# Sixteen batches split into parts of 12 and 4 instead of 10 and 6 for the last layer, with new groups and a new group order

## Chip, core and metric

One core of one Trainium2 chip runs the whole program in one launch. The metric is the device time of that core in microseconds (us), the median of the runs shown; smaller is better. Engines: PE multiplies matrices, PEld loads its weights, DVE, ACT and POOL work on vectors, SP issues most DMAs. DMAs between memory and memory, or memory and the on-chip buffers, run on 16 DMA engines that all queues share.

## What is computed

Input `x` has 16 batches of 256 tokens with 256 features, in f32. Four layers follow one another, each adding to `x`: a cross-attention with 8 heads, a feed-forward layer with per-batch weights, a second cross-attention, and a mixture of 8 experts. Only the last one matters here:

```
x = x + _L1_ffn_ref(_layernorm(x, axis=-1), Wg, Wu, Wd, Wr, temperature)

inh = sigmoid(x @ Wr / temperature)                       # one number per token and expert
in_zone = (inh >= 0.5 - log(4/3)) & (inh <= 0.5)
w = exp(-abs(inh - 1/e) / 0.1) * in_zone                  # no expert in zone: the two nearest serve
h = silu(gate) * up ; e_out = h @ Wd ; out = sum over e of weights_e * e_out_e
```

The reference lets each expert work on each token, and weights the result. The weight is zero where the expert does not serve the token, so how many tokens an expert serves depends on the data.

## The kernel before, in words

**Attention and chains.** The loop at L1297 has 128 steps, one per batch and head, with the matmuls of the first attention. What follows for a batch (output projection, feed-forward layer, second attention, last layer norm: `chain`) and its routing (`route`) are generators. Function `gap` runs them between the matmuls of the loop, by a model of the time that PE needs, so the order of instructions on each engine is fixed when the program is built.

**Routing.** `route` counts with two small matmuls (`pn`, L699) how many tokens each expert serves. It keeps a running count `next_slot` for each part and expert. A part is a set of consecutive batches: `PARTS = (10, 6)` (L161), so part 0 has 2560 tokens and part 1 has 1536 (`NTOKS`). Each token has one slot in the list of each expert, in a DRAM tensor `slots_d` per part: a served token takes the next slot from the front, any other a slot from the end. POOL scatters the rows there (L718), 16 scatters of 128 rows per batch.

**Capacity.** `CAPS` (L163) is half the tokens of a part: 1280 slots for part 0 and 768 for part 1. Only these first slots of each list are worked on in the normal course. A tile is 128 slots, so there are 8 x 10 + 8 x 6 = 128 tiles.

**Expert groups.** `groups` cuts lists into groups of up to four tiles: (4, 3, 3) for part 0, (3, 3) for part 1, and (3, 2, 1) for the last expert of part 1. `experts` (L1229) works on them in the order of `lists`. For a group, three groups ahead, SP loads its rows (L1137). Two groups ahead DVE transposes 32x32 blocks (L291), and SP sends them to DRAM and fetches them back in turned order (L296, L302), which completes the transposition. Then come `gate` (`pg`) and `up` (`pu`) with tanh on ACT and two DVE operations (L1205, L1206). One group later, `down` (`pd`) is scaled by the token's weight on DVE (`o`, L1219), and POOL adds each tile into the output with one scatter (L1220). There are nine `o` buffers. Scatters of one part and expert, and scatters of different parts, may overlap; a scatter of the same part but another expert waits until those before it have landed.

The first two groups of the job are prepared by PE transposes (`rowsT`, L84) instead of that round trip. The job starts four steps before the end of the loop, beside the last chains; a load from part 1 is not issued until batch 15 has been routed.

**The guarded block.** At the end DVE compares the counts with the capacities (`more_d`, `most`, `beyond`, L1356 to L1358). All engines load the result into a register (L1359) and branch on it (L1360). If any expert of any part has more tokens than its capacity, the block at L1361 works on all remaining slots of all lists, from the capacity to the end:

```
        nc.vector.tensor_tensor(more_d, next_slot, limit, ALU.subtract)
        nc.vector.tensor_reduce(most, more_d.rearrange("p k e -> p (k e)"), AX.X, ALU.max)
        nc.vector.tensor_scalar(beyond, most, 0.0, None, ALU.is_gt)
        some = nc.values_load(beyond[0:1, 0:1], min_val=0, max_val=1)
        with tc.If(some > 0):
            drain(experts(groups(0, "+", (4, 3, 3)) + groups(1, "+", (3, 3))))
```

Of the kernel before, what the change touches and what calls it, by code (L numbers as in the profile page):

```python
# [29 lines left out]
def xattn_ffn_kernel(  # L30
# [16 lines left out]
    E = Wg.shape[0]  # L47
# [110 lines left out]
    )  # L158


    PARTS = (10, 6)  # L161
    NTOKS = [n * S for n in PARTS]
    CAPS = [n // 2 for n in NTOKS]  # L163

# [151 lines left out]
    def advance(gen):  # L316
        return gen is not None and next(gen, DONE) is not DONE

    def drain(gen):
        while advance(gen):  # L320
            pass
# [306 lines left out]
    def route(b, A, mine):  # L628
        while not mine.done or (b >= 1 and not A.tails[b - 1].done):
            yield 0.4  # L630
        part = 0 if b < PARTS[0] else 1
        row = A.row[b]
# [105 lines left out]
    with ExitStack() as sh, ExitStack() as sa, ExitStack() as sf:  # L738
# [377 lines left out]
        def load_expert(e):  # L1116
            k = len(D_.w)
            pool = D_.front if k == 0 else D_.wk if k == 1 else D_.more
            w = D_.w[e] = pool.tile([P, 3, DC, D], F32, bufs=1, name=f"wx_{e}")
            nc.sync.dma_start(w[:, 0], Wg[e].rearrange("(c p) i -> p c i", p=P))  # L1120
            nc.sync.dma_start(w[:, 1], Wu[e].rearrange("(c p) i -> p c i", p=P))
            nc.sync.dma_start(w[:, 2], Wd[e].rearrange("(c p) d -> p c d", p=P))
# [106 lines left out]
        def experts(groups, ready=None):  # L1229

            if groups[0].e not in D_.w:
                load_expert(groups[0].e)
            for g in groups[:2]:
                g.load()
            yield 7.0
            while D_.wk is None:
                yield 0.4
            for d in range(DC):
                groups[0].turn_rows(d)
                yield 2.0  # L1240
            late = None
            for n, g in enumerate(groups):
                if n == 0:
                    groups[2].load()
                if n + 3 < len(groups):
                    while ready is not None and not ready(groups[n + 3]):
                        yield 0.4
                for i in range(IC):
                    g.gate(i)
                    yield  # L1250
                    g.up(i)
                    yield
                    if n == 0:
                        groups[1].turn_rows(i)
                    if n + 2 < len(groups):
                        if i == 0:
                            groups[n + 2].send_rows()
                        else:
                            groups[n + 2].fetch_rows()
                    if i == 0 and n + 3 < len(groups):  # L1260
                        groups[n + 3].load()
                    if late is not None:
                        late.down(2 * i)
                        late.down(2 * i + 1)
                        yield
                ahead = groups[min(n + 3, len(groups) - 1)].e
                if ahead not in D_.w and (len(D_.w) < 2 or D_.more is not None):
                    load_expert(ahead)
                if n + 2 < len(groups) and groups[n + 2].e not in D_.w:
                    while D_.more is None:  # L1270
                        yield 0.4
                    load_expert(groups[n + 2].e)
                late = g
            for t in range(late.tiles):
                late.down(t)

        def groups(part, more, sizes, experts_=range(E)):

            gs = []
            for e in experts_:  # L1280
                t = CAPS[part] // P if more else 0
                for k in sizes:
                    gs.append(G(part, e, t, k, more))
                    t += k
                assert t == NTOKS[part] // P if more else t == CAPS[part] // P
            return gs

        first = groups(0, "", (4, 3, 3))  # L1290
        lists = (
            first[:-1] + groups(1, "", (3, 3), range(E - 1))
            + first[-1:] + groups(1, "", (3, 2, 1), [E - 1])
        )

        last = None
        for n in range(NS + 2):  # L1297
# [60 lines left out]
        nc.vector.tensor_scalar(beyond, most, 0.0, None, ALU.is_gt)  # L1358
        some = nc.values_load(beyond[0:1, 0:1], min_val=0, max_val=1)  # L1359
        with tc.If(some > 0):  # L1360
            drain(experts(groups(0, "+", (4, 3, 3)) + groups(1, "+", (3, 3))))  # L1361


# [36 lines left out]
```

## Time and profile before

| | us |
|---|---|
| median of 3 runs | 1845.71 (1845.11 to 1851.59) |
| profiled execution, its time | 1845.63 |
| its span, first to last instruction | 1843.6 |
| PE busy | 1808.7 (98%) |
| DVE busy | 1212.0 (66%) |
| POOL busy | 846.4 (46%) |
| ACT busy | 583.2 (32%) |

The profiled execution took 1845.63 us, 2.0 us more than its span. Busy PE time includes waits inside its pipeline. In lines that tell of waiting, the engine after the arrow is the one whose result came last; `issue` means that nothing which the profile shows was waited for. Names that end in q are the sequencers of an engine.

### The profile page before, as it was taken

How to read it: one execution, taken by the hardware profiler on the slowest of the kernel's cores; microseconds unless marked ns; L12 is line 12 of the kernel's file. 1: busy time of each engine (PE TensorE's matmuls, PEld its weight loads, DVE VectorE, ACT ScalarE, POOL GpSimd, SP SyncE). 2: the span in 40 equal slices, each digit the busy share in tenths (PEclk: the TensorE clock that was granted, in tenths of full speed). 3: DMA queues.
4: the chain of work that ended last, by engine and by line, in shares of the span. 5: the costliest groups of instructions: out<-in, count | busy, mean ns of one | idle time of the engine just before them, and what ended most of it. 6: DMA issues, size and time to landing. Idle time of an engine off the chain costs nothing.

```text
span 1843.6 us, 22696 instructions
## 1 busy us (share of the span) xinstructions
PE 1808.7 (98%) x6600; PEld 1230.4 (67%) x6600; DVE 1212.0 (66%) x3349; ACT 583.2 (32%) x1298; POOL 846.4 (46%) x980
## 2 busy tenths in 40 slices
PE   8999999999999999999999999999999999999996
PEld 4666666666666666666667676767676676666664
DVE  5456585858585858586767676757566676655553
ACT  3443333333434333333333333333333321111110
POOL 2123235353535353535353535353524178766655
PEclk9999999999999999999999999999999999999998
DMA  6553546464646465645455556464636478999986
GB/s 223 180 183 121 165 148 203 153 201 153 205 146 205 161 197 161 195 156 198 161 193 164 190 164 197 154 204 146 202 103 222 133 215 193 238 242 225 214 204 100
DMA packets 271181, 332.72 MB, mean 180 GB/s; under 512 B 31388, under 2 KB 222792, under 8 KB 271048
## 3 DMA queue, kind: packets, MB, share of 16 engines
q1 hardware_dynamic: 240280, 279.63, 48.2%
q0 software_dynamic: 30720, 51.54, 12.2%
q8 instruction: 55, 0.90, 0.2%
q14 instruction: 78, 0.64, 0.1%
q10 hardware_dynamic: 48, 0.01, 0.0%
HBM read 165.77 MB, written 165.28 MB: 180 GB/s over the span
## 4 chain that ended last, share of the span: by engine, by line
PE 93%; DVE 3%; DMA 1%; issue 1%; POOL 1%; SPq 0%; ACT 0%; ACTq 0%; DVEq 0%; POOLq 0%
PE po L80 13%; PE pv L80 13%; PE sc L80 13%; PE pk L80 11%; PE pq L80 7%; PE px L80 6%; PE ph L80 6%; PE pg L80 6%; PE pf L80 6%; PE pu L80 5%; PE pd L80 5%; PE pl L80 1%; POOL out_dram L1220 0%; DVE tb L910 0%; PE pn L80 0%
## 5 line engine op out<-in xcount | busy, mean ns | idle before, releaser
L902 POOL TENSOR_SCALAR pr<-pr,ri 128x512 f32<-128x512 f32 x256 | 179.4, 711 | 319.5 <-DVE ri L901 314.5
L894 ACT ACTIVATE pr<-sc,nm 128x512 f32<-128x512 f32 x256 | 173.5, 682 | 478.3 <-DVE nm L888 405.9
L718 POOL DMA_INDIRECT slots_d<-row,at_slot x256 | 253.3, 989 | 70.4 <-issue 70.4
L1220 POOL DMA_INDIRECT out_dram<-o,at x128 | 201.2, 1572 | 100.6 <-issue 26.5
L80 PE MATMUL po<-pT,v 128*128 128x256 f32 x1024 | 242.1, 379 | 1.3 <-DVE W2T L955 0.7
L80 PE MATMUL sc<-kT,qT 128*128 128x512 f32 x512 | 241.1, 593 | 1.5 <-ACT kT L827 1.5
L80 PE MATMUL pk<-kvT,Wk_sb 128*128 128x512 f32 x512 | 240.6, 592 | 0.0
L80 PEld LDWEIGHTS po<-pT,v 128*128 128x128 f32 x1024 | 194.4, 190 | 69.2 <-issue 37.5
L80 PE MATMUL pv<-Wv_sb,kvT 128*128 128x512 f32 x512 | 235.2, 592 | 0.0
L940 DVE TENSOR_SCALAR outT<-po,cvec 128x256 f32<-128x256 f32 x128 | 61.0, 477 | 250.6 <-PE po L80 229.6
L910 DVE STREAM_TRANSPOSE tb<-pr 128x512 f32<-128x512 f32 x256 | 165.8, 685 | 6.9 <-DMA hop<-tb 6.5
L80 PEld LDWEIGHTS pv<-Wv_sb,kvT 128*128 128x128 f32 x512 | 97.1, 190 | 107.3 <-issue 102.1
L888 DVE TENSOR_REDUCE nm<-sc 128x1 f32<-128x512 f32 x256 | 160.2, 662 | 2.0 <-PE sc L80 1.9
L80 PEld LDWEIGHTS sc<-kT,qT 128*128 128x128 f32 x512 | 96.9, 190 | 70.1 <-issue 61.2
L80 PEld LDWEIGHTS pk<-kvT,Wk_sb 128*128 128x128 f32 x512 | 97.3, 190 | 67.8 <-issue 61.2
L80 PE MATMUL pg<-yTd,wx 128*128 128x384 f32 (+3 forms) x328 | 127.1, 510 | 7.9 <-DVE yTd L829 5.7
L80 PE MATMUL pq<-kvT,Wq_sb 128*128 128x256 f32 x512 | 132.8, 382 | 0.0
L1195 ACT ACTIVATE sg<-pg 128x384 f32<-128x384 f32 (+3 forms) x82 | 41.3, 503 | 278.3 <-PE pg L80 244.7
L80 PEld LDWEIGHTS pq<-kvT,Wq_sb 128*128 128x128 f32 x512 | 96.4, 191 | 42.1 <-issue 28.5
L80 PE MATMUL pd<-wx,hTd 128*128 128x256 f32 x512 | 123.9, 379 | 0.6 <-DVE hTd L1206 0.6
L80 PE MATMUL pu<-yTd,wx 128*128 128x384 f32 (+3 forms) x328 | 123.7, 500 | 0.0
L825 ACT COPY v<-pv 128x512 f32<-128x512 f32 (+1 forms) x132 | 70.6, 535 | 164.9 <-PE pv L80 163.9
(205 smaller groups left out, 2700.3 us busy)
## 6 DMA issues: line engine op xcount, KB each, us to landing
hop<-tb SPq DMA_DIRECT2D x128, 512.0 KB
pT<-hop SPq DMA_DIRECT2D x512, 128.0 KB
ev<-ev_d SPq DMA_DIRECT2D x32, 512.0 KB
rows<-slots_d SPq DMA_DIRECT2D x31, 397.5 KB
hop_rows_b<-rows_b SPq DMA_DIRECT2D x30, 384.0 KB
yTd<-hop_rows_b SPq DMA_DIRECT2D x120, 96.0 KB
rows<-slots_d SPq DMA_DIRECT2D x8, 530.0 KB
cin<-in_ctx_dram SPq DMA_DIRECT2D x16, 256.0 KB
```

What stands on the lines that cost most here:

```text
L80: nc.tensor.matmul(out, lhsT, rhs, **kw)
L718: ins = nc.gpsimd.indirect_dma_start(out=slots_d[part], out_offset=bass.IndirectOffsetOnAxis(ap=at_slot[:, c, e : e + 1], axis=0), in_=row ...
L825: nc.scalar.copy(out, src)
L888: nc.vector.tensor_reduce(nm, sc, AX.X, ALU.max, negate=True)
L894: nc.scalar.activation(pr, sc, AF.Exp, bias=nm, accum_out=sm)
L902: nc.gpsimd.tensor_scalar(pr, pr, ri, 1.0, ALU.mult, ALU.mult)
L910: nc.vector.transpose(tb[:, :, c, :], heads[n][c][0].rearrange("p (m f) -> p m f", m=QP))
L940: nc.vector.tensor_scalar(o, po, col("bv", h), None, ALU.add)
L1195: nc.scalar.activation(self.sg, self.pg, AF.Tanh, scale=0.5)
L1220: ins = nc.gpsimd.indirect_dma_start(out=out_rows[0 : sum(NTOKS[: self.part + 1]), :], out_offset=bass.IndirectOffsetOnAxis(ap=self.at[:, ...
```

## The change

The parts become 12 and 4 batches: 3072 and 1024 tokens, with capacities of 1536 and 512 slots. There are still 8 x 12 + 8 x 4 = 128 tiles. The lists of part 0 become three groups of four for experts 0 to 5, (3, 3, 3, 3) for expert 6 and (3, 3, 2, 2, 2) for expert 7; each list of part 1 is one group of four tiles. The last eight groups of part 0 are dealt out, one behind each group of part 1, so the order ends with part 1, part 0, part 1, part 0. Before, 41 groups; now 35. The guarded block's groups follow the new sizes: the slots behind the capacity are again 8 x 12 + 8 x 4 = 128 tiles, in 32 groups of four.

```diff
-    PARTS = (10, 6)
+    PARTS = (12, 4)
...
-        first = groups(0, "", (4, 3, 3))
-        lists = (
-            first[:-1] + groups(1, "", (3, 3), range(E - 1))
-            + first[-1:] + groups(1, "", (3, 2, 1), [E - 1])
-        )
+        first = groups(0, "", (4, 4, 4), range(E - 2))
+        first += groups(0, "", (3, 3, 3, 3), [E - 2]) + groups(0, "", (3, 3, 2, 2, 2), [E - 1])
+        second = groups(1, "", (4,))
+        lists, first = first[:-E], first[-E:]
+        for pair in zip(second, first):
+            lists += pair
...
-            drain(experts(groups(0, "+", (4, 3, 3)) + groups(1, "+", (3, 3))))
+            drain(experts(groups(0, "+", (4, 4, 4)) + groups(1, "+", (4,))))
```

## The prediction

> **What bounds the kernel now.** I read the busy time by stretches first, for the stage in which only experts are left:
>
> ```profile
> core 0: us, PE busy (x) PEld busy (x) DVE busy (x) ACT busy (x) POOL busy (x), PEclk, DMA share, GB/s
> 1700.00:1790.00 90.00, 90.00 (x327) 61.87 (x326) 53.47 (x140) 11.27 (x23) 57.66 (x37) 1.00 0.93 209
> ```
>
> PE is busy for 90.00 of 90 us at the full clock; POOL has 57.66 us, and the DMA engines are 93% busy. Only PE work, or a wait that stops PE, can move this stage.
>
> Then the chain of waits from 1590 us on, which has the PE work by itself:
>
> ```profile
> 1652.50 1.73 PE pd L80 x8
> 1654.23 1.72 PE pg L80 x4
> 1655.95 1.72 PE pu L80 x4
> ...
> 1670.93 4.13 DMA yTd<-hop_rows_b
> ...
> 1750.34 1.73 PE pd L80 x8
> 1758.09 1.73 PE pd L80 x8
> ```
>
> A four-tile group has 2 x 1.72 (`pg`), 2 x 1.72 (`pu`) and 2 x 1.73 us (`pd`): 10.34 us, 2.58 us a tile. A three-tile group recurs every 1758.09 - 1750.34 = 7.75 us, also 2.58 a tile. Group size is free on PE. The 4.13 us are a stall for rows that came back late.
>
> Last the end of the program, in the timeline and by source line:
>
> ```profile
> 1828.05 0.70 PE L80 MATMUL pd<-wx,hTd 128*128 128x256 f32 x2 [0.55 <-DVE hTd L1206]
> ...
> 1829.59 0.15 DVE L1358 TENSOR_SCALAR beyond<-most 128x1 int32<-128x1 f32 x1
> ...
> 1832.96 1.56 POOL L1220 DMA_INDIRECT out_dram<-o,at  x1 [0.30 <-issue]
> ```
>
> ```profile
> L1359 SPq TENSOR_LOAD <-beyond x1: 471/471/471, 1829.8 to 1829.8; - x1
> ...
> L1360 PEldq COMPARE_BRANCH  x1: 4400/4400/4400, 1830.4 to 1830.4; - x1
> ...
> L1360 SPq COMPARE_BRANCH  x1: 50/50/50, 1830.6 to 1830.6; - x1
> ```
>
> PE's last work ends at 1828.75, the last scatter at 1834.52, the span 9.08 us later at 1843.6. `beyond` is ready at 1829.74 and SP has branched at 1830.65. The guarded block does not run: the page counts 128 scatters into the output, one for each of the 128 tiles of the lists.
>
> **The regrouping by itself.** Tiles stay 128, scatters 128, and each tile costs PE 2.58 us in any group, so PE work changes by nothing. Two things could move. The stalls: from 1590 us to the end the chain shows 4.13 us for rows and one gap of 2.65 us, so at most 6.8 us is to be gained if new timing removes both; such a stall can as well come anew. I take zero, with -7 to +7. Part 1 is needed earlier: its first rows were requested at 1681.02, 23.7 us after batch 15's last scatter into the lists (1657.36). The first group of part 1 stood behind 77 tiles and now behind 75, and its load, three groups ahead, behind 64 instead of 67, so it comes 3 x 2.58 = 7.8 us sooner; some 16 us of cover stay, and the cost is nothing. Were that cover gone, SP would wait with all later row traffic behind it. Part 0 must wait for batches 10 and 11 as well, but the lists were last scattered into before the job's first load (1397.3) at 1290 to 1320 (batch 11) and from 1390 (batch 12, still part 1): some 77 us to spare. Dealing out part 0 between the groups of part 1 takes from POOL the wait at each expert change in part 1; PE did not wait for it before, so nothing is gained.
>
> **The capacity.** Here the change does something that is not in its lists. The tokens that an expert serves follow from the data. I evaluated the reference on its inputs up to the routing. Expert 0 serves, in batches 10 to 15, 115, 129, 129, 135, 118 and 134 tokens. Before, part 1 held all six: 760, under its 768 slots. Its fullest list in part 0 has 1099 of 1280. So no list overflows, as the trace says. Now part 1 is the last four: 129 + 135 + 118 + 134 = 516 tokens for 512 slots. It overflows by four, while every other list fits (452 of 512 at most; 1340 of 1536). One list is enough: `beyond` becomes 1 and the block runs for all experts and both parts, 8 x 12 + 8 x 4 = 128 more tiles, though four tokens need it.
>
> Is 516 safe against the chip's rounding? Of expert 0's 1024 routing values in these batches, 3 lie within 0.001 of an edge of the zone and 11 within 0.01. With errors of 0.01 drawn at random on all values the count stayed above 512 in 97% of draws; with 0.001 in all of them.
>
> **What the block costs.** Nothing runs beside it, so it adds in full:
>
> 1. Entry. SP issues the first rows at 1830.65. No row shows an unloaded load of this size; bounds: 530 KB at the 253 GB/s of the busiest stretch (1600 to 1650 us) is 2.1 us, plus the 2.1 us in which an unloaded scatter landed after its issue (1828.91 to 1831.05): 4.2. Two such loads go out together, which gives up to 6.3. I take 5.4, so 1836.0. Eight transposes took 1.04 us in all (1425.92), an ACT copy out takes about 0.6 each: first `pg` at 1838.2, which is 9.5 us after PE's last work.
> 2. Cold PE. After an idle time of 5.68 us the trace has this `pg`, of a size that takes 1.72:
>
> ```profile
> 1432.64 3.78 PE L80 MATMUL pg<-yTd,wx 128*128 128x512 f32 x4 [5.68 <-DVE yTd L829]
> ```
>
>    It lost 2.06 us, part of it a wait for its second operand. The Trainium skill (TensorE: Matmul & The Clock Gate, Part 1) halves the clock after some 3.4 us of idleness until some 3.4 us of work have passed: 1.7 us. I take the row, 2.1.
> 3. Branch. A rule speaks against any such block: the skill (Runtime: NRT & Kernel Launch, Instruction fetch mechanics) says that a taken branch out of the fetched window stalls until the target's page is fetched. Before, the jump past the block shows it: 4.40 us on PE. By the rule, falling into the block that follows the branch in program order costs nothing; by the row, if this stalled too, SP would issue some 3.5 us later. I take zero and keep 3.5 for the range.
> 4. Work: 128 x 2.58 = 330.7 us on PE, plus 1.0 for the second group's transposes. Bytes per tile are as before and the packets of four-tile groups are larger, so the DMA share should not pass 0.93. Row stalls like the 4.13 us may come back once or twice: zero, up to 8.
> 5. Tail. The block's last 8 groups are part 1, one group per expert, so each group's first scatter waits until the last of the one before has landed. POOL's timeline shows this wait at each change of expert in part 1, for example
>
> ```profile
> 1768.25 1.55 POOL L1220 DMA_INDIRECT out_dram<-o,at  x1 [0.30 <-DVE o L1219]
> 1775.08 1.56 POOL L1220 DMA_INDIRECT out_dram<-o,at  x1 [5.27 <-DMA out_dram<-o,at]
> ```
>
>    Six such gaps from 1724 to 1806 us have a mean of 4.7. With six scatters between changes that took 6 x 1.86 + 4.4 = 15.6, and PE gave 15.5: just hidden. With four it takes 4 x 1.56 + 3 x 0.30 + 4.7 = 11.8 against PE's 10.34, so POOL falls back 1.5 us a group. PE has nine `o` buffers and is not stopped by a lag of four tiles, but the end moves. Following POOL through these 8 groups, with 4.7 us for each landing and 2.1 for the last, its last scatter ends 15.4 us after PE's last work, against 1834.52 - 1828.75 = 5.8 before. Without the waits for landing (2.1 each) it is 9.0; with 5.5 each 19.5.
>
> Sum, against the profiled execution: 1828.75 + 9.5 + 2.1 + 1.0 + 330.7 + 15.4 + 9.1 = 2196.5 of span, plus 2.0 around it: 2198.5 us. The profiled 1845.63 stands 0.1 from the median, so I forecast 2198.5.
>
> **The rivals.**
>
> *The block runs and PE alone sets its end.* POOL's landings come sooner, since the end of the block has fewer transfers in flight: tail 6 to 9 us instead of 15.4, 2189 to 2192. For it: unloaded scatters landed in 2.1 us. Against: at this pace the DMA engines are 93% busy up to three groups before the end.
>
> *The block runs and the rows come late.* In the block all rows go through the same round trip, with no attention to cover it at the start; if each of the 8 experts met one stall of 4.13 us, 33 us come on top: 2231. For it: the stall at 1670.93. Against: between 1700 and 1790 us, with the same bytes per tile, PE lost nothing.
>
> *The block does not run, so the change is not slower.* If the chip's count of expert 0 in the last four batches is 512 or less, four tokens fewer, `beyond` stays 0 and only the regrouping is left: 1845.6 - 7 to + 7, likeliest 1843 by removing part of the 6.8 us of stalls. That point decides alone, and it is worth 350 us. For it: the margin of four. Against: almost no values lie near the zone's edges.
>
> **How the numbers follow.** Differences under about 0.5% of the time, 9 us, cannot be told from none by measuring this kernel. Block with POOL's tail 0.63 (2198.5), with PE's end 0.20 (2190), with late rows 0.11 (2231), no block 0.06 (1843). The first two and their unknown terms span 2182 (tail -6.4, entry -1, regrouping -7, rounded) to 2222 (tail +4, branch 3.5, entry 1, rows 8, regrouping 7): this leaves out about 0.17. Slower by over 0.5%: 0.94. Without the block the time lies within 0.5% but for the best end of its stalls: same 0.05, faster 0.01.
>
> **What would show it.** The block is told by 256 scatters into the output instead of 128, and a branch on PE of well under 4.40 us. The entry is the idle time of PE before `rowsT` and the first `pg` of the block (9.5 us from the last `pd`), the cold clock that `pg`'s length. The pace is 10.34 us between groups; the tail, the time from PE's last `pd` to the last scatter. The regrouping is right if PE reaches the branch at 1829 within 7 us. All of it falls if 128 scatters are counted.

## The result: the block runs, and the time rises by 340 us

The changed kernel takes 2186.14 us, the median of 4 runs (2185.54 to 2187.68), against 1846.29 for the kernel before in the same session (4 runs, 1845.11 to 1851.59). The ratio is 1.1835, with a 95% interval of [1.1811, 1.1859]. The profiled execution took 2187.68 us, with a span of 2185.9.

Its page has twice the scatters into the output and 946 more matmuls (7546 records; before 6600). The last line is that of the kernel before:

```profile
span 2185.9 us, 25784 instructions
...
PE 2144.8 (98%) x7546; PEld 1412.6 (65%) x7546; DVE 1399.5 (64%) x3752; ACT 621.4 (28%) x1354; POOL 1043.2 (48%) x1108
...
L1220 POOL DMA_INDIRECT out_dram<-o,at x256 | 397.4, 1552 | 249.8 <-DVE o L1219 175.7
```

```profile
L1220 POOL DMA_INDIRECT out_dram<-o,at x128 | 201.2, 1572 | 100.6 <-issue 26.5
```

By source line, the branch (now L1361) comes twice on each engine, on the way in and at the block's end. On PE it takes 87 to 180 ns; the jump past the block took 4400 ns before:

```profile
L1361 PEldq COMPARE_BRANCH  x2: 87/134/180, 1829.5 to 2165.1; - x2
...
L1361 SPq COMPARE_BRANCH  x2: 38/44/49, 1829.8 to 2145.1; - x2
```

The timeline of the changed kernel has the way into the block. The first column is the start, the second the length, and brackets hold the idle time before it:

```profile
1824.28 3.62 PE L80 MATMUL pd<-wx,hTd 128*128 128x256 f32 x16
...
1829.87 7.66 SPq L1137 DMA_DIRECT2D rows<-slots_d  x3
1835.17 1.97 PE L84 MATMUL rowsT<-ident,rows 128*128 128x128 f32 x8 [7.27 <-DMA rows<-slots_d]
...
1836.96 2.65 PE L80 MATMUL pg<-yTd,wx 128*128 128x512 f32 x4
```

PE ends its lists at 1827.90, so the first `pg` of the block starts 9.06 us later. Within the block, two stretches have the same columns as the first view of the prediction:

```profile
1860.00:1900.00 40.00, 40.00 (x125) 23.52 (x124) 23.08 (x56) 4.78 (x8) 24.03 (x16) 1.00 0.89 210
...
2050.00:2100.00 50.00, 50.00 (x157) 29.64 (x156) 29.27 (x70) 5.37 (x9) 29.56 (x20) 1.00 0.87 203
```

PE is busy in every microsecond at the full clock. The DMA engines are 87 to 89% busy, less than the 93% of the lists before. The end of the block in the timeline, DVE's and POOL's lines alone:

```profile
2159.66 0.48 DVE L1219 TENSOR_SCALAR o<-pd,wt 128x256 f32<-128x256 f32 x1 [0.18 <-PE pd L80]
...
2161.64 1.54 POOL L1220 DMA_INDIRECT out_dram<-o,at  x1 [2.99 <-DVE o L1219]
...
2164.82 0.48 DVE L1219 TENSOR_SCALAR o<-pd,wt 128x256 f32<-128x256 f32 x1 [0.18 <-PE pd L80]
...
2165.58 1.54 POOL L1220 DMA_INDIRECT out_dram<-o,at  x1 [0.55 <-DVE o L1219]
...
2167.43 1.54 POOL L1220 DMA_INDIRECT out_dram<-o,at  x1 [0.30 <-issue]
...
2169.14 0.48 DVE L1219 TENSOR_SCALAR o<-pd,wt 128x256 f32<-128x256 f32 x1 [0.38 <-PE pd L80]
2172.01 1.54 POOL L1220 DMA_INDIRECT out_dram<-o,at  x1 [3.04 <-DMA out_dram<-o,at]
...
2177.55 1.54 POOL L1220 DMA_INDIRECT out_dram<-o,at  x1 [0.30 <-issue]
```

A group starts to scatter 10.37 us after the one before it (2172.01 - 2161.64). At a change of expert POOL waits for the landing of the scatter before, though the profile names `o` at most of these places. At 2172.01 the landing is named, and every `o` had been ready since 2169.62. At 2161.64 the wait is as long, and the tile's own `o` had been ready since 2160.14, 1.5 us before; the third scatter of that group began 0.28 us after its `o` (2165.30). PE's last work ends at 2169.09, the last scatter at 2179.09, the span 6.8 us after that.

### The profile page after: what moved, and what is told of

It reads as the page before. It is cut to its first block, busy times and chain, and to the rows that moved or that the text cites. A ratio compares the mean times of both kernels' runs of the same rounds, so it can differ in the third digit from the quotient of the medians.

```text
span 2185.9 us, 25784 instructions
## 1 busy us (share of the span) xinstructions
PE 2144.8 (98%) x7546; PEld 1412.6 (65%) x7546; DVE 1399.5 (64%) x3752; ACT 621.4 (28%) x1354; POOL 1043.2 (48%) x1108
## 3 DMA queue, kind: packets, MB, share of 16 engines
q0 software_dynamic: 49152, 68.32, 15.7%
## 4 chain that ended last, share of the span: by engine, by line
PE 96%; DVE 2%; DMA 1%; issue 0%; POOL 0%; ACT 0%; POOLq 0%; ACTq 0%; SPq 0%; DVEq 0%
PE pv L80 11%; PE po L80 11%; PE sc L80 11%; PE pg L80 10%; PE pu L80 10%; PE pd L80 10%; PE pk L80 10%; PE pq L80 6%; PE px L80 5%; PE pf L80 5%; PE ph L80 5%; PE pl L80 1%; POOL out_dram L1220 0%; DVE tb L910 0%; PE pn L80 0%
## 5 line engine op out<-in xcount | busy, mean ns | idle before, releaser
L1220 POOL DMA_INDIRECT out_dram<-o,at x256 | 397.4, 1552 | 249.8 <-DVE o L1219 175.7
L80 PE MATMUL pg<-yTd,wx 128*128 128x512 f32 (+2 forms) x536 | 244.6, 579 | 5.7 <-DVE yTd L829 5.7
L1195 ACT ACTIVATE sg<-pg 128x512 f32<-128x512 f32 (+2 forms) x134 | 77.5, 578 | 584.6 <-PE pg L80 555.0
L80 PE MATMUL pu<-yTd,wx 128*128 128x512 f32 (+2 forms) x536 | 242.7, 575 | 0.0
L80 PE MATMUL pd<-wx,hTd 128*128 128x256 f32 x1024 | 242.1, 379 | 0.0
L80 PEld LDWEIGHTS pd<-wx,hTd 128*128 128x128 f32 x1024 | 194.3, 190 | 72.7 <-issue 48.8
L1205 DVE SCALAR_TENSOR_TENSOR sg<-sg,pg 128x512 f32<-128x512 f32 (+2 forms) x134 | 89.0, 664 | 189.3 <-ACT sg L1195 176.1
L80 PEld LDWEIGHTS pu<-yTd,wx 128*128 128x128 f32 x536 | 102.1, 191 | 115.9 <-issue 98.2
L80 PEld LDWEIGHTS pg<-yTd,wx 128*128 128x128 f32 x536 | 101.9, 192 | 73.8 <-issue 55.1
```

Of the source, the lines that this page charges most:

```text
L80: nc.tensor.matmul(out, lhsT, rhs, **kw)
L1195: nc.scalar.activation(self.sg, self.pg, AF.Tanh, scale=0.5)
L1205: nc.vector.scalar_tensor_tensor(sg, sg, 1.0, self.pg, ALU.add, ALU.mult)
L1220: ins = nc.gpsimd.indirect_dma_start(out=out_rows[0 : sum(NTOKS[: self.part + 1]), :], out_offset=bass.IndirectOffsetOnAxis(ap=self.at[:, ...
```

## The experiments

Three things were to be told apart: whether the block is the whole loss, what entry, work and tail cost in it, and what the new order of the lists does without the block.

**1. Does the block do all of it?** The threshold is raised above and below four tokens. With 4.5 the block stays out, and expert 0's share for four tokens is left out.

```diff
-        nc.vector.tensor_scalar(beyond, most, 0.0, None, ALU.is_gt)
+        nc.vector.tensor_scalar(beyond, most, 4.5, None, ALU.is_gt)
```

> The changed kernel with one number altered: the guarded block is entered only if a list overflows by more than 4.5 tokens, so the four tokens of expert 0 that have no slot before the capacity miss that expert's share. Theory (the block is the whole loss, and the overflow is 516 - 512 = 4): the block is not entered, 128 scatters, PE's last work at 1827.9 as in the changed kernel's trace, last scatter at 1833.4, then about 9.1 us to the end as before: span 1842.5, time 1844.5 (1842 to 1847), a regrouping worth -1 us. Rival A (the new groups or their order cost the time): 2186, nothing gained back. Rival B (the overflow is larger than worked out, or sits in another list): the block runs, 2186.

> The changed kernel with the block entered if a list overflows by more than 3.5 tokens; what is computed is complete. Theory: the chip's count is 516, an overflow of 4, so the block runs: 256 scatters, 2186 us. Rival (the chip's count differs by rounding and the overflow is 3 or less): the block is not entered, about 1844.5. With the run at 4.5 this fixes the chip's count to one token.

With 4.5: 1844.56 us (22 runs) against 1848.3 (27 runs), ratio 0.9979 [0.9971, 0.9987]; 128 scatters. With 3.5: 2184.83 us in one run; 256 scatters. So the overflow lies between 3.5 and 4.5: the chip counts 516 tokens for 512 slots, as was worked out. The block is the whole loss; without it the new split and order are 0.2% faster.

**2. Does the block's price depend on the new split?** In the kernel before, the threshold becomes -10000.0, so its block always runs, with the groups of the parts of 10 and 6.

> The kernel before (10 and 6 batches, old groups), with the threshold so low that its own guarded block is always entered; the added rows have weight zero, so what is computed is complete. Theory (the block costs entry plus 128 tiles at PE's pace whatever the split): 1828.75 + 9.1 entry + 1.5 cold and transposes + 330.2 work + about 8 to the last scatter + 6.8 to the end = 2184.4 of span, 2186 us (2180 to 2195), the same as the changed kernel. Its part 1 has two groups of three tiles per expert, so POOL's gap at a change of expert tells whether 3.0 us (as in the changed kernel's block) or 4.7 us (as in the lists before) belongs to group size: if packets of 768 bytes make the landing slow, 4.5 or more; if not, about 3. Rival (the block is dear only with the new split): clearly below 2170.

It took 2184.88 us (4 runs), ratio to the kernel before 1.1827 [1.1809, 1.1846], as expected. The 128 tiles cost the same with the old split. In POOL's timeline the waits at the change of expert in part 1, here behind six scatters, are longer than in the changed kernel:

```profile
2072.07 1.55 POOL L1220 DMA_INDIRECT out_dram<-o,at  x1 [3.87 <-DMA out_dram<-o,at]
...
2087.60 1.55 POOL L1220 DMA_INDIRECT out_dram<-o,at  x1 [3.90 <-DMA out_dram<-o,at]
...
2118.84 1.55 POOL L1220 DMA_INDIRECT out_dram<-o,at  x1 [4.14 <-DMA out_dram<-o,at]
```

Six of them have a mean of 4.1 us, between the two values expected, at a DMA share of 0.93 (2040 to 2150 us, 207 GB/s). The seven between experts of part 1 in the changed kernel are 2.9 to 3.3, with a mean of 3.0. There the DMA share is 0.87 from 2100 to 2150 us and 0.39 from 2150 to the end.

**3. Is it the smaller pieces that make this wait longer?** The rows of a three-tile group move in pieces of 768 bytes, those of four tiles in 1024. In the changed kernel, part 1 of the block is cut into pairs, with pieces of 512 bytes and the same four scatters per expert.

```diff
-            drain(experts(groups(0, "+", (4, 4, 4)) + groups(1, "+", (4,))))
+            drain(experts(groups(0, "+", (4, 4, 4)) + groups(1, "+", (2, 2))))
```

> The changed kernel with the block's groups of part 1 cut into two of two tiles each, so that an expert still has four tiles but rows travel in pieces of 512 bytes instead of 1024. Theory (the wait for landing at a change of expert grows with smaller pieces, since they load the DMA engines more: 3.0 us with pieces of 1024, 4.1 with 768): gaps of 4.5 us or more between experts at the end of the block, a DMA share over 0.93 there, and POOL falling behind: tail 15 to 22 us instead of 10.0, 2190 to 2200 us. Rival (the wait does not depend on piece size): gaps of about 3.0 and a time of 2183 to 2188.

One run, 2187.34 us. Six of the waits were 3.5 to 4.0 us, 3.84 in the mean, and the last one 3.08; for example

```profile
2139.45 1.54 POOL L1220 DMA_INDIRECT out_dram<-o,at  x1 [3.85 <-DVE sg L1205]
```

and the stretch around it shows the DMA engines no busier than with whole groups, and PE losing 2.88 of 60 us:

```profile
2100.00:2160.00 60.00, 57.12 (x259) 48.27 (x258) 36.36 (x109) 8.04 (x21) 32.61 (x22) 1.00 0.87 191
```

The time lies where an unchanged wait would have it, but the waits are longer than that, and shorter than the other expectation. The tail, for which 15 to 22 us were expected, was 4.2: PE's last work ended at 2174.69, 5.6 us later than in the changed kernel, and the last scatter at 2178.89, almost where it was (2179.09). So the edit moved PE's work too, and is no clean test of the pieces. Each byte does take more of the DMA engines in smaller pieces: 0.87 at 203 GB/s, 0.93 at 207, 0.87 at 191 are 0.43, 0.45 and 0.46 of their time per 100 GB/s.

The DMA queues tell more. Queue q1 carries the rows and the fetches of `yTd`, q0 the scatters. Here is the share of the DMA engines that q1 had from the end of one expert's last scatter to the start of the next one's first. The kernel before (1769.80 to 1775.08 us, a wait of 5.27) comes first, then the changed kernel (2127.69 to 2130.58, 2.89), experiment 2 (2114.70 to 2118.84, 4.14) and experiment 3 (2135.59 to 2139.45, 3.85):

```profile
q1 hardware_dynamic: 977, 0.80, 55.0%
```

```profile
q1 hardware_dynamic: 8, 0.00, 0.8%
```

```profile
q1 hardware_dynamic: 720, 0.79, 66.7%
```

```profile
q1 hardware_dynamic: 727, 0.53, 45.2%
```

In the changed kernel's block the row traffic falls between the waits: q1 has 0 to 9% in all seven of them. At the last change of experiments 2 and 3, behind the last rows, q1 has nothing, and the waits are 3.0 and 3.1 there too. So about 3.0 us is what the wait takes without rows beside it, and the longer ones have rows beside them. The DMA share of the stretch does not set it: around the wait of 2.89 us (2120 to 2140) it is 0.90. No run moved the row traffic alone, so this is read from the traces and not shown by an experiment, and it is not the whole rule: in the first version of experiment 6 a wait was 3.31 us with q1 at 54%.

**4. What does the way in cost, if the jump is taken?** One guarded block for each part; only part 1's runs, 32 tiles instead of 128. All engines jump over part 0's block and fall into the second.

```diff
...
-        some = nc.values_load(beyond[0:1, 0:1], min_val=0, max_val=1)
-        with tc.If(some > 0):
-            drain(experts(groups(0, "+", (4, 4, 4)) + groups(1, "+", (4,))))
+        for k, sizes in enumerate(((4, 4, 4), (4,))):
+            some = nc.values_load(beyond[0:1, k : k + 1], min_val=0, max_val=1)
+            with tc.If(some > 0):
+                drain(experts(groups(k, "+", sizes)))
```

> The changed kernel with one guarded block per part in place of one for both, each entered only if a list of its own part overflows; what is computed is complete. Theory (the block costs its entry plus 2.58 us per tile, wherever it is): only part 1's block runs, 8 x 4 = 32 tiles and 160 scatters: 1827.9 + 9.1 entry + 1.5 cold and transposes + 32 x 2.58 = 82.6 + 10.0 tail + 6.8 to 9.1 end = 1939 of span, 1941 us (1935 to 1950), so 245 us less than the changed kernel. Rival (the loss is one of the branch and of code loading, not of tiles): within 50 us of 2186.

1943.77 us (4 runs), ratio 1.0517 [1.05, 1.0533], as expected. It is 242.4 us less than the changed kernel; 96 tiles of 2.58 are 247.7, so the second branch took about 5 us back. By source line, PE's taken branch is 4958 ns:

```profile
L1362 PEldq COMPARE_BRANCH  x2: 82/2520/4958, 1829.3 to 1834.9; - x2
```

SP's own branches took 43 and 55 ns, yet its first rows left at 1834.44, 4.57 us later than in the changed kernel. Its list of waits (total, times, longest) says why:

```profile
SPq L1137 <- DVEq L1362: 2.2, 1, 2.2
...
SPq L1137 <- PEq L1362: 0.8, 1, 0.8
```

SP may not write row buffers before DVE and PE are past their own jumps. The slowest engine's jump holds up the loads.

**5. A fifth tile for the one list that overflows.** Expert 0 of part 1 gets 640 slots as groups of three and two tiles; the block stays out. Part 1 begins behind 18 groups of part 0 in this kernel, and behind 19, as in the changed kernel, in the next.

```diff
+    TILES = [[c // P] * E for c in CAPS]
+    TILES[1][0] += 1
...
+    nc.gpsimd.memset(limit[:, 1, 0:1], float(TILES[1][0] * P))
...
-        second = groups(1, "", (4,))
-        lists, first = first[:-E], first[-E:]
+        second = groups(1, "", (3, 2), [0]) + groups(1, "", (4,), range(1, E))
+        lists, first = first[: -E - 1], first[-E - 1 :]
         for pair in zip(second, first):
...
```

> The changed kernel with a fifth tile for expert 0 of part 1 (640 slots, groups of three and two tiles), so that 516 tokens fit; block kept for all that lies behind. Theory: no block; 129 tiles instead of 128, so 2.6 us of PE more than the run with the threshold at 4.5: 1847 us (1844 to 1850), level with the kernel before. Rival A (the split or the order costs the time): 2186 plus 3.

1854.8 us (6 runs), ratio 1.0044 [1.0029, 1.006]: a miss by 8 us. SP's timeline:

```profile
1651.64 0.34 SPq L299 DMA_DIRECT2D hop_rows_b<-rows_b  x1
1664.81 0.38 SPq L1140 DMA_DIRECT2D rows<-slots_d  x1
```

SP stands for 12.8 us at part 1's first load. The chain of waits names what it stood for, batch 15's last scatter into the lists, and PE's timeline what that cost:

```profile
1662.21 2.58 DMA slots_d<-row,at_slot
...
1664.81 5.22 DMA rows<-slots_d
```

```profile
1672.06 3.75 PE L80 MATMUL pg<-yTd,wx 128*128 128x512 f32 x4 [5.30 <-DVE o L1222]
1675.61 2.59 PE L80 MATMUL pu<-yTd,wx 128*128 128x512 f32 x4
1678.03 1.89 PE L80 MATMUL pd<-wx,hTd 128*128 128x256 f32 x8
```

The next fetch of `yTd` left only behind that load, at 1665.27. From start to start `pg` took 3.55 us and `pu` 2.42, where each takes 1.72 in an undisturbed stretch: 2.5 us of cold PE. With 5.3 of stall and 2.6 for the tile that is 10.4, against the 10.2 us that this kernel takes more than experiment 1.

With part 1 one group later:

```diff
-        lists, first = first[: -E - 1], first[-E - 1 :]
-        for pair in zip(second, first):
+        lists, first = first[:-E] + second[:1], first[-E:]
+        for pair in zip(second[1:], first):
...
```

> The kernel with five tiles for expert 0 of part 1 again, but with the first group of part 1 behind 19 groups of part 0 as in the changed kernel, not 18. The run before lost 5.3 us on PE and then ran at half clock, because SP waited with the first load of part 1 until batch 15's last scatter had landed. Theory (that load's cover is short by about one group): no stall at 1672, 129 tiles, 2.6 us more than the run at 4.5: 1847 us (1845 to 1850), a complete result without the block. Rival (the fifth tile or the three-and-two split costs 10 us by itself): 1855.

1847.41 us (13 runs) against 1847.38 for the kernel before (17 runs), ratio 1.0 [0.9992, 1.0009], as expected. The stall is gone. So part 1's place in the changed kernel is the earliest that PE does not pay for, to within one group.

**6. Versions that beat both.** If capacities may be fitted to these counts, lists can be shorter. First per list, with the guarded block kept for what lies behind:

```diff
+    TILES = [[11, 10, 9, 10, 10, 10, 9, 11], [5, 3, 4, 4, 4, 4, 3, 4]]
...
+        lists = first[:-3] + second[:-1] + first[-3:-2] + second[-1:] + first[-2:]
...
```

> Parts of 12 and 4 with the capacity of each list set to the tiles that its count needs (part 0: 11, 10, 9, 10, 10, 10, 9, 11; part 1: 5, 3, 4, 4, 4, 4, 3, 4), 111 tiles instead of 128; the first group of part 1 behind 69 tiles of part 0; the block is kept for all that lies behind. Theory (time is tiles times 2.58 us, and nothing else is near): 17 x 2.58 = 43.9 us less than the run at 4.5 with its 1844.6: 1801 us (1798 to 1808), faster than both kernels. Rival (shorter lists uncover the last chain or the DMAs, which become the bound): above 1815.

1808.9 us (5 runs), ratio 0.9791 [0.9778, 0.9805], with 111 tiles instead of 128; 8 us above what was expected. PE's last work ends at 1783.45, the last scatter at 1797.18: a tail of 13.7 us, against 5.5 in experiment 1. Here part 1's groups follow one another, and POOL waits at each, as the prediction had feared for the block:

```profile
1741.83 1.54 POOL L1221 DMA_INDIRECT out_dram<-o,at  x1 [3.99 <-DVE o L1220]
...
1752.73 1.54 POOL L1221 DMA_INDIRECT out_dram<-o,at  x1 [3.82 <-DVE sg L1206]
...
1763.11 1.54 POOL L1221 DMA_INDIRECT out_dram<-o,at  x1 [3.31 <-DMA out_dram<-o,at]
```

Then the last list of part 0 is cut into (2, 2, 2, 2, 1, 1, 1) and five of these groups are dealt out between those of part 1.

> The 111-tile kernel with expert 7's list of part 0 in groups of 2, 2, 2, 2, 1, 1, 1, the last five of them dealt between the groups of part 1. In the run before, PE was done at 1783.5 as worked out, but POOL's last scatter ended 13.7 us later, where the run at 4.5 had 5.5: consecutive groups of part 1 each waited 3.3 to 4.2 us for the landing of the last expert's scatter. Theory (these waits are the 8 us that the run before missed): tail of 6 to 8 us and 1801 to 1804 us. Rival (the small groups stall PE by as much, or the tail is something else): 1807 to 1812.

1808.43 us (5 runs), ratio 0.9794 [0.9773, 0.9816]: no gain over the version without it, as the rival had it. The tail did fall to 5.4 us. But PE's last work came 10.0 us later (1793.48), because its waits for rows rose. In the list of waits of the version without dealing, then of the one with it:

```profile
PE pg L80 <- DMA yTd<-hop_rows_b: 1.5, 2, 1.2
```

```profile
PE pg L80 <- DMA yTd<-hop_rows_b: 7.9, 4, 4.0
```

The longest wait stands at 1777.81, behind groups of one tile. Three groups of lead are less time when groups are short, and the row round trip no longer fits; that is how I read the place of this wait, and no run tests it.

Last the old parts of 10 and 6, with nine tiles per list of part 0 (1152 slots for at most 1099 tokens), 120 tiles, and part 1 behind all of part 0.

```diff
-    CAPS = [n // 2 for n in NTOKS]
+    CAPS = [9 * P, 6 * P]
...
-        first = groups(0, "", (4, 3, 3))
         lists = (
-            first[:-1] + groups(1, "", (3, 3), range(E - 1))
-            + first[-1:] + groups(1, "", (3, 2, 1), [E - 1])
+            groups(0, "", (3, 3, 3), range(E - 1)) + groups(0, "", (3, 2, 2, 2), [E - 1])
+            + groups(1, "", (3, 3), range(E - 1)) + groups(1, "", (3, 2, 1), [E - 1])
...
```

> The split of before (10 and 6 batches) with a capacity of nine tiles instead of ten for part 0, one number for all experts (1152 slots; its fullest list has 1099), and part 1 begun behind all of part 0, with expert 7 as 3, 2, 2, 2. Theory (8 tiles fewer at 2.58 us, no list overflows, the load of part 1 issued behind 66 tiles stays covered): 20.6 us less than before, less what POOL's waits leave behind at the end (0 to 3): 1826 us (1823 to 1831). Rival (part 1 without part 0 groups between, or the earlier load, gives it back): 1835 or more.

1830.27 us (6 runs), ratio 0.99 [0.9885, 0.9915], inside the range expected. So with no new split at all a tighter capacity gains 1%.

## Why the prediction held, step by step

**Capacity.** Right. The overflow of four tokens, worked out from the reference's routing, is the chip's own (experiment 1), and it decides 340 us.

**Work.** Right: from the first `pg` to the end of the last `pd` 332.1 us, of which 0.8 are cold PE (below), so 331.4 against 330.7 + 1.0, with PE busy throughout. No row stall came back, so the rival "rows come late" (2231) falls.

**Entry.** Right: 9.06 us against 9.5. The rows landed 5.25 us after their issue (5.4 taken). The register load and the branch, from the last `pd` to the issue, took 1.97 us (1.90).

**Branch.** Right: falling through cost 0.09 to 0.18 us on PE, next to nothing, as the Trainium skill (Runtime: NRT & Kernel Launch, Instruction fetch mechanics) has it for code that follows in program order. Experiment 4 has the other side, the taken jump, and shows that it counts on each engine that holds a buffer.

**Cold PE.** The mechanism held, the size did not: `pg` took 2.48 us in the chain of waits, 0.76 over 1.72, where 2.1 was taken. But the eight transposes ahead of it took 1.97 us against 1.04. So part of the cold time lay in them, inside the entry. The granted clock (third column from the end) agrees:

```profile
1832.00:1836.00 4.00, 0.83 (x4) 0.84 (x5) 0.24 (x2) 0.00 (x0) 1.43 (x1) 0.50 1.06 281
1836.00:1840.00 4.00, 4.00 (x12) 2.26 (x11) 0.00 (x0) 1.52 (x3) 0.00 (x0) 0.71 0.60 140
```

Half clock until 1838.3 gives the 0.71 of the second stretch, so only the first 1.4 us of `pg` were at half clock. In experiment 4, after 11.58 us of idleness, the same `pg` took 3.55 us in the chain of waits.

**Tail.** The term that was mis-sized: 10.0 us measured, 15.4 predicted. The mechanism was right: each expert's first scatter waits for a landing. The size was wrong: the step took 4.7 us for each landing, from groups in the lists before, and in the block it was 3.0. Four scatters and a wait then take 4 x 1.54 + 3 x 0.30 + 3.0 = 10.1 us. PE gives 10.3, so POOL does not fall behind by 1.5 us a group, as the step had it; with 4.7 it would have. The 15.4 does not follow from the step's own figures either: 9.0 us and six changes at 1.5 each are 18.

On the pace the rival "PE alone sets its end", given 0.20, was right: POOL is held to PE's pace, by about 0.2 us a group, at the third scatter. Its sum of 2189 to 2192 is nearer too. On the end it was not: 10.0 us lie above its 6 to 9, since the last group's first scatter waits for a landing until 2172.01, when every `o` has been ready for 2.4 us. Its reason, that transfers become fewer at the end, is not what made the waits short. They were 3.0 us before the last rows had gone, at a DMA share of 0.90 (2120 to 2140), and after, at 0.43 (2150 to 2172). What the traces have in its place is that next to no row traffic ran during these waits (experiment 3). Why it fell between them, and whether it alone makes the 4.7 of the lists, stays open. That the fear itself was sound is seen in the fitted lists of experiment 6, where waits of 3.3 to 4.0 made the tail 13.7 us.

**End.** 6.8 us against 9.1. Where the block is jumped over, POOL has an instruction of 1294 ns behind its last scatter (at L1360 of the kernel before) that is missing here; the other microsecond is not settled, as the end varies from 7.5 to 10.4 us among the kernels that jump.

**Sum.** 1827.90 + 9.06 + 332.1 + 10.0 + 6.8 = 2185.9. Against the prediction: tail -5.4, end -2.3, cold -1.3, end of the lists -0.85, entry -0.4, work -0.3 are the 10.6 us by which the span is shorter. The time of 2186.14 lies near the low end of the range, 2182, and the terms named for that end add to 2184 (2198.5 - 6.4 - 1 - 7).

**Regrouping.** Taken as zero, with 7 to each side; it gave 0.2% (experiment 1). But two of its readings were wrong. First, "4.13 us were a stall" took a piece of the chain for idle time of PE. A DMA piece in the chain has the length of the transfer. PE's own list of waits in the kernel before, from 1590 us to the end of the lists, has

```profile
PE pg L80 <- DVE o L1219: 1.9, 1, 1.9
PE pd L80 <- DVE hTd L1206: 0.6, 1, 0.6
PE pg L80 <- DMA yTd<-hop_rows_b: 0.3, 1, 0.3
```

so at most 2.8 us could be won, not 6.8; in experiment 1 that list is empty. Second, "some 16 us of cover stay" used the wrong load. In the kernel before, 1681.02 is the next group's; part 1's first left at 1673.04, 15.7 us after batch 15's last scatter (1657.36). The changed kernel's SP timeline shows what was left of it:

```profile
1664.39 0.34 SPq L296 DMA_DIRECT2D hop_rows_b<-rows_b  x1
1670.45 0.37 SPq L1137 DMA_DIRECT2D rows<-slots_d  x1
```

The last scatter into the lists came at 1664.51, 7.2 us later than before, and SP stood 5.7 us at the load. PE did not stall, so the price was indeed nothing; but the cover was used up, and experiment 5 shows it at work one group earlier, 5.3 us of stall and 2.5 of cold PE.

## What to carry to other kernels

Where a kernel has a fixed capacity and a guarded fallback, a new split is first of all a new count against a new limit: work the count out from the data before any schedule, since four tokens cost 340 us here and all the rest of the change 4. Take an engine's idle time from its own waits, not from the length of a transfer in the chain, and name the one load or scatter that a cover is measured from. A lead counted in groups shrinks with the groups.

## What the runs showed of the hardware

A taken branch over a large block cost PE 4.40 us in the kernel before and 4.96 in experiment 4, and SP there only some 0.5 (from its branch at 1829.5 to its next instruction at 1830.0). Falling through cost 0.04 to 0.18 us on any engine of the changed kernel. A scatter that had to wait for another's landing waited 2.9 to 3.3 us in the changed kernel's block, where the row queue had 0 to 9% of the DMA engines meanwhile, and 3.5 to 5.5 us in the kernel before and in experiments 2 and 3, where it had 40 to 68%. After 7.27 us of idleness PE's transposes took 1.97 us instead of 1.04, at a granted clock of 0.50, so the cold time begins with them, not with the first large matmul.
